# Attention's last chunks on one Trainium2 core: side columns copied ahead of one-hot matrices, one-hot matrices made by GpSimd, and residual sums placed behind the last gather

## The chip, the cores and the metric

The kernel runs on one core of one Trainium2 chip. The core has five engines that each work through their own queue in order: TensorE (PE, with its weight loads as PEld), VectorE (DVE), ScalarE (ACT), GpSimd (POOL) and SyncE (SP). They meet at semaphores. ACT, DVE and POOL compute on tiles of 128 partitions; POOL also issues the indirect DMAs (gathers) of this kernel, and SP issues its plain loads and stores. PE writes to PSUM, a small memory of banks; the other tiles live in SBUF.

The metric is the device time of one execution in microseconds. The kernel before takes 6164.96 us (median of 3 runs, 6163.35 to 6166.92).

## The reference, cut to what matters

A graph network with 6250 nodes of 128 features and 200,000 edges, sorted by destination. Two convolutions over the edges come first; then attention, whose end the change touches:

```python
q = (h @ qw + qb).reshape(n, H, HD)          # H = 8 heads, HD = 16
k = (h @ kw + kb).reshape(n, H, HD)
v = (h @ vw + vb).reshape(n, H, HD)
logits = (q[dst] * k[src]).sum(-1) * scale + (edge_attr @ ew + eb)
amax = jax.ops.segment_max(logits, dst, num_segments=n)
pe = jnp.exp(logits - amax[dst])
ssum = jax.ops.segment_sum(pe, dst, num_segments=n)
w = pe / jnp.clip(ssum[dst], 1e-06)
o = jax.ops.segment_sum(w[:, :, None] * v[src], dst, num_segments=n)
o = o.reshape(n, D) @ ow + ob
o = group_norm(o, an_g, an_b)
return h + o                                  # and the caller adds x
```

## The kernel before

**Chunks.** The edges are cut into 1563 columns of 128, and 8 columns make a chunk: 196 chunks, numbered 0 to 195, the last with 3 columns. For each chunk `fetch` (L1511) issues one plain load on SP and 8 gathers on POOL (L718, one indirect DMA of 128 rows of k and v for each column) into `k.g`, a ring of 11 buffers. The two convolutions before attention gather in the same way.

**First half of a chunk, in edge order.** PE multiplies the chunk's query rows with a one-hot matrix `ohT`, which ACT makes from loaded positions (`compared`, L685 and L686): the product `qe` has each edge's query and bias. `logits` multiplies it with the gathered keys on DVE (L1391), reduces over each head (L1395) and adds the bias `ebs`, which ACT copies out of PSUM (L1393), on DVE (L1397).

**Groups.** Chunks are grouped by 8, and at the end by 6, 5, 4 and 3 (`TAILS`, L37): 178 to 183, 184 to 188, 189 to 192 and 193 to 195. When a group's logits are there, `maxima` (L1409) turns them on PE (L1420), runs two scans on DVE (L1423, L1424), turns back (L1428), subtracts (L1432), takes the exponent on ACT (L1434, tile `pe`) and makes the end-of-run maxima `wl` on DVE (L1435).

**Second half, for the chunks of a finished group.** It runs one or two chunks a step, spread over the steps that the next group takes. For a chunk it needs
- a one-hot matrix `k.oh` of 128x1024 (edge by node of the window). DVE makes it in one instruction (L733, 173 times). For 23 chunks of the last 26 (`BY_ACT = 26`, L38) ACT makes it instead, a step ahead, in `early` (L1531): 8 squares (L1498) and one Relu (L1499);
- the tile `k.v` (`values`, L1572): ACT copies `pe` into every 17th column (L1444, inside `weighted`), DVE multiplies the gathered values with `pe` (L1445), and ACT copies `wl` and the end marks into 9 side columns (L1574, L1575). There are two buffers of `v`;
- the sums: 8 matmuls of `k.oh` with `k.v` on PE (L1452) into one of two PSUM tiles `us`;
- a merge with the running maxima `M` (`merge_late`, L1481: five small DVE instructions L1485, L1488, L1459, L1461, L1462, a copy L1463, and two exponents on ACT, L1465 and L1467), and one step later `add_late` (L1469 to L1477) into the running sums `flat`.

**What sets the order.** `pipeline` (L821) writes the steps out; `in_order` then fixes DVE, SP, ACT and PE to the order in which the Python code emits. POOL is not in that list (`ORDERED`, L17): a scheduler places its instructions by their dependencies. In step `n` the emitted order is: the fetch of chunk n+2, the second halves (`second`, L1541), the first half of chunk n, `values_ahead` for the next chunk (L1577), `compared` for chunk n+2, the products of chunk n+1, `early`, and then the piece of a batch of finished nodes (`attention_nodes`: copies `n_x` L908 and squares L919 on ACT, and others).

**After the chunks.** The last 9 windows of nodes need residuals: `h2` and `x` rows are loaded (`residuals`, L1016), `an_b` is added on POOL (L1606, one instruction of 128x1152), and x is added on POOL (`add_x`, L1027 and L1029). `last_nodes(3, hx[0])` then finishes those windows on DVE, ACT and PE.

Of the kernel before, what the change touches and what calls it, by code (L numbers as in the profile page):

```python
# [8 lines left out]
FP = mybir.dt.float32  # L9
# [3 lines left out]
ALU = mybir.AluOpType  # L13
# [8 lines left out]
P = 128  # L22
D = 128
H = 8
HD = 16
NT = 1
CH = NT * P
TPC = 8
# [22 lines left out]
def kernel(ctx: ExitStack, tc: tile.TileContext, x, src, dst, eat, w, out):  # L51
# [663 lines left out]
    def gather(k, g, table_d, ring=None):  # L715
        behind = None
        for t in range(k.nt):
            h = nc.gpsimd.indirect_dma_start(  # L718
                out=g[:, t, :table_d.shape[1]], out_offset=None, in_=table_d,
                in_offset=bass.IndirectOffsetOnAxis(ap=k.src[:, t:t + 1], axis=0))  # L720
            if ring is None:
                continue
            if behind is not None:
                tc.add_manual_dep(
                    h.ins, behind.name,
                    mybir.DependencyInfo(mybir.DependencyClass.NoSync, mybir.DependencyReason.DATA),
                    reason="one ring's order")
            behind = h.ins
            ring.mark(h, k.c, t, k.nt - 1)

    def onehot(k, pools, iota):
        k.oh = pools["oh"].tile([P, TPC, P], FP, name="oh")
# [609 lines left out]
    with ExitStack() as es:  # L1342
# [66 lines left out]
        def maxima(run, lg, nb, bp):  # L1409
# [27 lines left out]
            for j, k in enumerate(run):  # L1437
                k.pe, k.wl = pe[:, :k.nt, j, :], wl[:, :k.nt, j, :]

        def weighted(k):  # L1440

            k.v = vp.tile([P, TPC, VK + H + 1], FP, name="v", bufs=2)
            v4 = k.v[:, :, :VK].rearrange("p t (h c) -> p t h c", c=HD + 1)
            nc.scalar.copy(v4[:, :k.nt, :, HD], k.pe)  # L1444
            nc.vector.tensor_tensor(  # L1445
                v4[:, :k.nt, :, :HD], k.g[:, :k.nt, D:].rearrange("p t (h c) -> p t h c", c=HD),
                k.pe[:, :, :, None].to_broadcast([P, k.nt, H, HD]), ALU.mult)
# [47 lines left out]
        def onehot_by_act(k):  # L1495
# [2 lines left out]
                nc.scalar.activation(k.oh[:, t, :], iota_j, AF.Square, bias=k.dm[:, t:t + 1], scale=-1.0)  # L1498
            nc.scalar.activation(k.oh[:, :k.nt, :], k.oh[:, :k.nt, :], AF.Relu, bias=1.0, scale=-1.0)  # L1499

        class Stage:
            ahead, soon = 2, False
            sums, late, nb = [], [], None
# [7 lines left out]
            def fetch(self, c):  # L1511
                k = loads(c, pools, a_d[3], self.ahead)
                k.g = gp.tile([P, TPC, KV], FP, name="g")
                gather(k, k.g, kv_d, ring)
                return k

            def products(self, k):
# [12 lines left out]

            def early(self, ks, n, then):  # L1531

                for c in then[:2]:
                    if c >= NCH - BY_ACT:
                        onehot_by_act(ks[c])

            def root(self, run):
# [3 lines left out]
            def second(self, run, ks, first):  # L1541


                pieces = iter(())
                if run:
                    pieces = maxima(run, self.lg, self.nb, self.bp)
                    self.nb, self.j = None, 0
                for n, k in enumerate(ks):
                    mine = pieces if n == len(ks) - 1 else iter(())
                    next(mine, None)  # L1550
                    if k.oh is None:
                        onehot(k, pools, iota_of(k))
                    if self.sums:
                        self.sums[0].win = wins[self.sums[0].c]
                    next(mine, None)


                    if self.late:
                        add_late(self.late.pop(0))
                    if k.v is None:  # L1560
                        self.values(k)
                    sums(k, VK + H + 1)
                    next(mine, None)
                    self.values_ahead(ks[n + 1:] or self.then)
                    if self.sums:
                        merge_late(self.sums[0])
                        self.late.append(self.sums.pop())
                    self.sums.append(k)
                self.pieces = pieces
                return True  # L1570

            def values(self, k):  # L1572
                weighted(k)
                nc.scalar.copy(k.v[:, :k.nt, VK:VK + H], k.wl)  # L1574
                nc.scalar.copy(k.v[:, :k.nt, VK + H], ef[:, k.c * TPC:k.c * TPC + k.nt])  # L1575

            def values_ahead(self, ks):  # L1577

                for k in ks[:1]:
                    if k.pe is not None and k.v is None:  # L1580
                        self.values(k)

            def finish(self):
# [14 lines left out]
                add_late(self.sums[0])  # L1598

        with tc.tile_pool(name="bpa", bufs=1) as bp, tc.tile_pool(name="ohTa", bufs=2) as pools["ohT"]:  # L1600
            pipeline(3, Stage(bp))

        n = NW - NWD
        whole = min(n, FULL - NWD)
        hx = residuals(fin, NWD, n, whole, pool("xr", 1))
        nc.gpsimd.tensor_tensor(hx[0], hx[0], rows["an_b"][:, None, :].to_broadcast([P, n, D]), ALU.add)  # L1606
        add_x(nc.gpsimd, hx[0], hx[1], whole, n)

        pools["left"] = pool("left", 1)
# [3 lines left out]
        def left(k):  # L1613
            lp = pools["left"]
            left_rows(k, pools, a_d[3], bank)
            k.c = 0
            k.g = gp.tile([P, TPC, KV], FP, name="g")
            gather(k, k.g, kv_d)
            products(k, [(k.ohf.rearrange("p t e -> p (t e)"), k.rows), (k.ea, webl)])
            lg = lp.tile([P, TPC, H], FP, name="l_lg")  # L1620
            logits(k, lg)
            neg = lp.tile([P, 4, P], FP, name="l_neg")
            part = lp.tile([P, H, 2], FP, name="l_part")
            junk = lp.tile([P, 4, P], FP, name="l_junk")
            for a in range(2):
                nc.vector.tensor_scalar(neg, k.ohf[:, 4 * a:4 * a + 4, :], 1.0, BIG, ALU.subtract, ALU.mult)
                for h in range(H):
                    bc = bank()
                    for t in range(4):
                        nc.tensor.transpose(bc[:, t, :], lg[:, 4 * a + t, h:h + 1].to_broadcast([P, P]), ident)  # L1630
                    nc.vector.tensor_tensor_reduce(
                        junk, bc, neg, 1.0, -BIG, ALU.add, ALU.max, part[:, h, a:a + 1])
            cm = lp.tile([P, H], FP, name="l_cm")
            nc.vector.tensor_reduce(cm, part, AX.X, ALU.max)
            me = ps_.tile([P, TPC, H], FP, name="l_me", tag="pe")
            for t in range(TPC):
                nc.tensor.matmul(me[:, t, :], lhsT=k.ohf[:, t, :], rhs=cm, start=True, stop=True)
            nc.vector.tensor_tensor(lg, lg, me, ALU.subtract)

            nc.vector.tensor_scalar(lg, lg, 0.0, None, ALU.min)  # L1640
            k.pe = lp.tile([P, TPC, H], FP, name="l_pe")
            nc.scalar.activation(k.pe, lg, AF.Exp)
            weighted(k)
            sums(k, VK)
            tt = t3[:, bass.ds(k.win, 1), :]
            merge(k, M[:, bass.ds(k.win, 1), :], None, cm[:, None, :], 1)
            add(k, tt, 1)
# [43 lines left out]
```

## Time and profile before

| what | number |
|---|---|
| median of 3 runs | 6164.96 us |
| the profiled execution's own time | 6177.55 us |
| its span | 6175.8 us |
| mean granted PE clock | 0.75 |
| gathers on POOL, both convolutions | 3126, 950 ns each |
| gathers on POOL, attention | 1563, 954 ns each |
| last gather issued | 6064.52 us from the start |

The profile is of one execution. The groups give, for instructions of one line, engine and shape, the busy time, the mean duration and the idle time of the engine just before them with what ended it. The timeline gives single instructions: start, duration, engine, line, operation, tiles, count, and in brackets the idle time before. All times below are microseconds from the start of the span unless they say otherwise. The profiled execution took 12.6 us longer than the median of the runs.

### The profile page before, as it was taken

Reading aid. Unit: us, or ns where it says so; the run is one execution under the profiler, and the core shown is the slowest. Engines: PE = TensorE matmul, PEld = TensorE weight load, DVE = VectorE, ACT = ScalarE, POOL = GpSimd, SP = SyncE. Lnnn points to the kernel's source line nnn. Section 1 sums busy time; section 2 is a strip of 40 time slices with the busy share of each in tenths; the row PEclk is TensorE's granted clock in tenths of the full one; section 3 lists DMA queues with packets and bytes.
Section 4 is the critical chain, followed back from the end, with each engine's and each line's share of the span. In section 5 each row is a group of like instructions: output and inputs, shape, how many; then the busy total and the mean of one; then the engine's idle time right before and its main releaser. Section 6 shows DMA issues by size and latency. Waiting matters only on the chain. (4 is left out here: it accounts for less than half of the span.)

```text
span 6175.8 us, 68330 instructions
## 1 busy us (share of the span) xinstructions
PE 3615.7 (59%) x20941; PEld 3418.9 (55%) x20942; DVE 4994.3 (81%) x7118; ACT 3353.9 (54%) x5295; POOL 4487.6 (73%) x4706
## 2 busy tenths in 40 slices
PE   5555556556556455565565656555655666666555
PEld 4555555555555455555555555544555555555555
DVE  7888888888888578777888888856778888888877
ACT  5666666666666566666666666632333333333354
POOL 5777777777777577777777777757777777777772
PEclk8777667777777677777777787766778777777776
DMA  6444344444433333343344444445566666666652
GB/s 160 116 127 121 96 115 105 102 108 107 107 101 101 80 100 96 100 101 100 102 114 114 109 112 108 112 121 146 152 157 162 165 166 163 163 166 162 165 150 62
DMA packets 391221, 758.87 MB, mean 123 GB/s; under 512 B 89647, under 2 KB 256946, under 8 KB 361441
## 3 DMA queue, kind: packets, MB, share of 16 engines
q0 software_dynamic: 175056, 410.03, 25.9%
q1 hardware_dynamic: 210144, 340.73, 21.0%
q10 hardware_dynamic: 5632, 3.50, 0.2%
q8 instruction: 173, 2.83, 0.2%
q14 instruction: 216, 1.77, 0.1%
HBM read 707.34 MB, written 46.58 MB: 122 GB/s over the span
## 5 line engine op out<-in xcount | busy, mean ns | idle before, releaser
L718 POOL DMA_INDIRECT g<-b_d,src_i x3126 | 2970.9, 950 | 963.4 <-issue 915.5
L1198 PE MATMUL u<-h,oh 128*128 128x129 f32 (+1 forms) x6252 | 1266.3, 384 | 1435.0 <-ACT h L1193 1434.9
L1198 PEld LDWEIGHTS u<-h,oh 128*128 128x128 f32 x6252 | 1169.3, 288 | 1517.1 <-ACT h L1193 1512.6
L718 POOL DMA_INDIRECT g<-kv_d,src_i x1563 | 1490.7, 954 | 494.6 <-issue 446.4
L1166 PE MATMUL m<-pk,ohT 101*128 101x128 f32 x6252 | 943.2, 315 | 206.4 <-DVE h L1173 161.9
L1166 PEld LDWEIGHTS m<-pk,ohT 101*128 101x128 f32 x6252 | 909.7, 231 | 227.3 <-DVE h L1173 180.7
L1173 DVE TENSOR_TENSOR h<-m,g 128x1024 f32<-128x1024 f32 x392 | 476.4, 1215 | 519.4 <-DMA g<-b_d,src_i 496.0
L1452 PE MATMUL us<-v,oh 128*128 128x145 f32 x3126 | 593.1, 359 | 385.4 <-DVE flat L1477 340.6
L1376 PE MATMUL qe<-pk,ohT 101*128 101x136 f32 x3126 | 567.1, 352 | 373.7 <-ACT ebs L1393 364.1
L1452 PEld LDWEIGHTS us<-v,oh 128*128 128x128 f32 x3126 | 549.8, 250 | 425.6 <-DVE flat L1477 239.6
L1376 PEld LDWEIGHTS qe<-pk,ohT 101*128 101x128 f32 x3126 | 525.0, 252 | 406.5 <-ACT ebs L1393 399.8
L1193 ACT ACTIVATE h<-h 128x1024 f32<-128x1024 f32 x392 | 413.0, 1054 | 594.4 <-DVE h L1192 578.9
L1175 ACT ACTIVATE sq<-h 128x1024 f32<-128x1024 f32 x392 | 411.7, 1050 | 527.9 <-DVE h L1173 526.0
L685 ACT ACTIVATE ohT<-ohT,minus_p 96x1024 f32<-96x1024 f32 x588 | 669.2, 1138 | 17.0 <-DMA ohT<-rel_d 16.5
L686 ACT ACTIVATE ohT<-ohT 96x1024 f32<-96x1024 f32 x588 | 619.8, 1054 | 18.7
L1177 DVE TENSOR_REDUCE var<-sq 128x64 f32<-128x1024 f32 x392 | 475.0, 1212 | 104.5 <-ACT sq L1175 104.4
L1191 DVE TENSOR_TENSOR h<-h,cps 128x1024 f32<-128x1024 f32 x392 | 477.1, 1217 | 13.5
L1192 DVE TENSOR_TENSOR h<-h,cps 128x1024 f32<-128x1024 f32 x392 | 477.0, 1217 | 13.4
L733 DVE TENSOR_TENSOR oh<-cps,dm 128x1024 f32<-128x1024 f32 x392 | 474.2, 1210 | 2.1 <-PE u L1198 2.1
L1188 DVE TENSOR_TENSOR h<-h,cps 128x1024 f32<-128x1024 f32 x392 | 473.7, 1208 | 0.0
L1391 DVE TENSOR_TENSOR g<-qe,g 128x768 f32<-128x768 f32 (+1 forms) x391 | 251.1, 683 | 235.0 <-DMA g<-kv_d,src_i 234.6
L1465 ACT ACTIVATE us<-d 128x16 f32<-128x16 f32 x196 | 36.7, 187 | 660.0 <-DVE d L1461 605.6
(286 smaller groups left out, 4270.6 us busy)
## 6 DMA issues: line engine op xcount, KB each, us to landing
ohT<-rel_d SPq DMA_DIRECT2D x291, 768.0 KB
g<-b_d,src_i POOLq DMA_INDIRECT x3126, 2.5
pk<-a_d SPq DMA_DIRECT2D x588, 46.0 KB
g<-kv_d,src_i POOLq DMA_INDIRECT x1563, 3.0
ohT<-in_eat_dram SPq DMA_DIRECT2D x291, 40.0 KB
a_d<-n_o SPq DMA_DIRECT2D x28, 256.0 KB
kv_d<-n_o SPq DMA_DIRECT2D x28, 256.0 KB
n_h<-h_d SPq DMA_DIRECT2D x19, 256.0 KB
```

Source lines behind the costliest of these rows:

```text
L685: nc.scalar.activation(k.ohT[:WN, :], k.ohT[:WN, :], AF.Square, bias=minus_p[:WN])
L686: nc.scalar.activation(k.ohT[:WN, :], k.ohT[:WN, :], AF.Relu, bias=1.0, scale=-4.0)
L718: h = nc.gpsimd.indirect_dma_start(out=g[:, t, :table_d.shape[1]], out_offset=None, in_=table_d, in_offset=bass.IndirectOffsetOnAxis(ap=k. ...
L733: return nc.vector.tensor_tensor(k.oh[:, :k.nt, :], iota[:, None, :].to_broadcast([P, k.nt, P]), k.dm[:, :, None].to_broadcast([P, k.nt, P ...
L1166: nc.tensor.matmul(k.m[:, t, :], lhsT=lhs[:, t * P:(t + 1) * P], rhs=rhs, start=(j == 0), stop=(j == len(terms) - 1))
L1173: nc.vector.tensor_tensor(k.mt, k.m[:, :n], k.g[:, :n], ALU.add)
L1177: return lambda: nc.vector.tensor_reduce(var[:, at:at + n * H], sq[:, :n].rearrange("p t (g c) -> p (t g) c", c=HD), AX.X, ALU.add)
L1191: nc.vector.tensor_tensor(k.mt, k.mt, over_edges(gam, k.nt), ALU.mult)
L1192: nc.vector.tensor_tensor(k.mt, k.mt, over_edges(bet, k.nt), ALU.add)
L1198: nc.tensor.matmul(k.u[:, 0, :wide], lhsT=k.oh[:, t, :], rhs=k.h[:, t, :wide], start=(t == 0), stop=(t == k.nt - 1))
L1376: nc.tensor.matmul(k.qe[:, t // TB, at:at + DB], lhsT=lhs[:, t * P:(t + 1) * P], rhs=rhs, start=(j == 0), stop=(j == len(terms) - 1))
L1452: nc.tensor.matmul(k.u[:, :wide], lhsT=k.oh[:, t, :], rhs=k.v[:, t, :wide], start=(t == 0), stop=(t == k.nt - 1))
```

## The change

Three edits, all in attention.

**1. Side columns.** `weighted` is split: `columns(k)` takes a buffer of `v` and copies `pe` into it, and the stage's `columns` adds the `wl` and end-mark copies. `early` calls it for the chunk after the last one whose values are done (`done + 1`), ahead of the one-hot matrices that it emits. `done` replaces the test on `k.v`. On ACT this changes the order alone: wherever the three copies stood behind the one-hot matrices or behind a batch's `n_x` copy or squares, they now stand ahead of them. That is so at 34 places in the middle of attention (behind `n_x` alone) and in nearly all steps of the last 26 chunks. The order on PE, DVE and SP is the same as before.

**2. One-hot matrices by GpSimd.** In the last three steps with chunks (n + 2 >= 195) `early` calls `onehot_by_pool`: 8 instructions of 128x128 on POOL for each chunk, tied behind the last gather that has been emitted. In the built program these are 4 chunks, 189 to 192, so 32 instructions; the 4 chunks' 36 instructions on ACT are gone. The last three, 193 to 195, are still made by DVE (L733), as before.

**3. Residual sums.** The sum of `an_b` on POOL is tied behind the last gather. Before, the scheduler had put it among the gathers, behind the 105th gather of attention; now the order on POOL is: last gather, sum of `an_b`, the 32 one-hot instructions, sums of `x`.

```diff
@@ gather
             behind = h.ins
             ring.mark(h, k.c, t, k.nt - 1)
+        return behind
+
+    def follows(h, behind):
+        tc.add_manual_dep(
+            h.ins, behind.name,
+            mybir.DependencyInfo(mybir.DependencyClass.NoSync, mybir.DependencyReason.DATA),
+            reason="behind the gathers")
+        return h
@@ values of a chunk
-        def weighted(k):
-
-            k.v = vp.tile([P, TPC, VK + H + 1], FP, name="v", bufs=2)
-            v4 = k.v[:, :, :VK].rearrange("p t (h c) -> p t h c", c=HD + 1)
-            nc.scalar.copy(v4[:, :k.nt, :, HD], k.pe)
+        def heads(k):
+            return k.v[:, :, :VK].rearrange("p t (h c) -> p t h c", c=HD + 1)
+
+        def columns(k):
+            k.v = vp.tile([P, TPC, VK + H + 1], FP, name="v", bufs=2)
+            nc.scalar.copy(heads(k)[:, :k.nt, :, HD], k.pe)
+
+        def weighted(k):
+            v4 = heads(k)
             nc.vector.tensor_tensor(
@@ one-hot matrices
+        def onehot_by_pool(k, behind):
+            k.oh = pools["oh"].tile([P, TPC, P], FP, name="oh")
+            for t in range(k.nt):
+                follows(nc.gpsimd.tensor_scalar(
+                    k.oh[:, t, :], iota_j, k.dm[:, t:t + 1], None, ALU.is_equal), behind)
@@ fetch
-                gather(k, k.g, kv_d, ring)
+                self.behind = gather(k, k.g, kv_d, ring)
@@ early
+                k = ks.get(self.done + 1)
+                if k is not None and k.pe is not None:
+                    self.columns(k)
                 for c in then[:2]:
-                    if c >= NCH - BY_ACT:
+                    if n + self.ahead >= NCH - 1:
+                        onehot_by_pool(ks[c], self.behind)
+                    elif c >= NCH - BY_ACT:
                         onehot_by_act(ks[c])
@@ second
-                    if k.v is None:
+                    if k.c > self.done:
                         self.values(k)
@@ values, values_ahead
+            done = -1
+
+            def columns(self, k):
+                if k.v is None:
+                    columns(k)
+                    nc.scalar.copy(k.v[:, :k.nt, VK:VK + H], k.wl)
+                    nc.scalar.copy(k.v[:, :k.nt, VK + H], ef[:, k.c * TPC:k.c * TPC + k.nt])
+
             def values(self, k):
+                self.columns(k)
                 weighted(k)
-                nc.scalar.copy(k.v[:, :k.nt, VK:VK + H], k.wl)
-                nc.scalar.copy(k.v[:, :k.nt, VK + H], ef[:, k.c * TPC:k.c * TPC + k.nt])
+                self.done = k.c
...
-                    if k.pe is not None and k.v is None:
+                    if k.pe is not None and k.c > self.done:
                         self.values(k)
@@ after the chunks
-            pipeline(3, Stage(bp))
+            stage = Stage(bp)
+            pipeline(3, stage)
...
-        nc.gpsimd.tensor_tensor(hx[0], hx[0], rows["an_b"][:, None, :].to_broadcast([P, n, D]), ALU.add)
+        follows(nc.gpsimd.tensor_tensor(
+            hx[0], hx[0], rows["an_b"][:, None, :].to_broadcast([P, n, D]), ALU.add), stage.behind)
@@ chunks outside the steps
+            columns(k)
             weighted(k)
```

## The prediction

> **What bounds the kernel now.** I read the table of stretches first, then DVE's groups in the stretch before the ACT one-hot matrices and in the stretch with them, then the timeline around the last.
>
> ```profile
> core 0: us, PE busy (x) PEld busy (x) DVE busy (x) ACT busy (x) POOL busy (x), PEclk, DMA share, GB/s
> 5000.00:5800.00 800.00, 488.46 (x2823) 455.71 (x2822) 685.39 (x1418) 288.39 (x775) 606.50 (x635) 0.79 0.63 164
> 5900.00:6066.00 166.00, 101.37 (x527) 94.10 (x527) 117.81 (x267) 102.41 (x289) 125.53 (x132) 0.71 0.57 151
> 6066.00:6155.00 89.00, 50.82 (x267) 46.72 (x266) 68.12 (x166) 43.78 (x137) 2.77 (x2) 0.71 0.08 21
> ...
> L1391 DVE TENSOR_TENSOR g<-qe,g 128x768 f32<-128x768 f32 x79 | 75.3, 954 | 58.0 <-DMA g<-kv_d,src_i 57.6 <-PE us L1452 0.3
> L1423 DVE TENSOR_TENSOR_SCAN blk<-nbs,blk 64x1024 f32<-64x1024 bf16 x10 | 22.9, 2287 | 18.3 <-PE blk L1420 18.3
> ...
> L718 POOL DMA_INDIRECT g<-kv_d,src_i x132 | 125.6, 951 | 40.2 <-issue 38.1 <-DVE flat L1477 0.6 <-DVE blk L1423 0.6
> L1445 DVE TENSOR_TENSOR v<-g,pe 128x1024 f32<-128x1024 f32 x25 | 30.5, 1220 | 52.1 <-ACT v L1444 52.1
> L1391 DVE TENSOR_TENSOR g<-qe,g 128x768 f32<-128x768 f32 x17 | 16.2, 951 | 0.0
> ```
>
> From 5000 to 5800 DVE has 85% of the time busy, and what it waits for is gathered rows (57.6 us, L1391). POOL issues gathers without a stop: 635 in 800 us, one every 1.26 us. So POOL's issue sets the pace. From 5900 to the end (the last three rows) L1391 waits no more: rows lie ready. DVE now waits 52.1 us ahead of L1445, for the side-column copies on ACT, and falls behind. At 6066 the gathers are over and DVE still needs 89 us. A wait in this last stretch is paid in full, and a gap in the gathers before it too.
>
> **Residual sum (edit 3).**
>
> ```profile
> 4217.99 0.95 POOL L718 DMA_INDIRECT g<-kv_d,src_i  x1 [0.30 <-issue]
> 4226.06 2.62 POOL L1606 TENSOR_TENSOR n_h<-n_h,r_an_b 128x1152 f32<-128x1152 f32 x1 [7.12 <-issue]
> 4228.86 1.19 POOL L718 DMA_INDIRECT g<-kv_d,src_i  x1 [0.18 <-issue]
> ...
> 6064.52 0.94 POOL L718 DMA_INDIRECT g<-kv_d,src_i  x1 [0.30 <-issue]
> ```
>
> A gather ends at 4218.94 and the next starts at 4228.86: 9.92 us where 0.30 is usual. The page does not say what the 7.12 us were; they leave the gather stream either way, so all later gathers, and with them DVE until 5900, come 9.6 us earlier. That is term A, **9.6 us**. Bounds: 2.6 if the 7.12 us return within the gathers, 9.9 at most. Its load of `h2` on SP does not move. It passes 1458 gathers on POOL and is needed only by the last sums on DVE, so at its new place it can only hold up what is queued behind it: the one-hot matrices (below) and the sums of x, which wait for a later load in any case.
>
> **Side columns (edit 1).** In the middle of attention the swap with a batch's copy changes nothing: DVE's wait for rows covers it, and without that cover it would be worth 0.5 us a place. In the last stretch there are two kinds of steps. A step with one ACT one-hot matrix:
>
> ```profile
> 6068.90 2.43 ACT L1498 ACTIVATE oh<-iota_j,dm 128x128 f32<-128x128 f32 x8
> 6071.36 1.06 ACT L1499 ACTIVATE oh<-oh 128x1024 f32<-128x1024 f32 x1
> 6072.61 1.22 DVE L1445 TENSOR_TENSOR v<-g,pe 128x1024 f32<-128x1024 f32 x1 [2.93 <-ACT v L1444]
> 6077.28 0.23 DVE L1397 TENSOR_TENSOR lg<-l,ebs 128x64 f32<-128x64 f32 x1
> ...
> 5951.62 1.22 DVE L1445 TENSOR_TENSOR v<-g,pe 128x1024 f32<-128x1024 f32 x1 [1.20 <-ACT v L1444]
> 6012.67 1.22 DVE L1445 TENSOR_TENSOR v<-g,pe 128x1024 f32<-128x1024 f32 x1 [4.56 <-ACT v L1444]
> 6082.55 1.22 DVE L1445 TENSOR_TENSOR v<-g,pe 128x1024 f32<-128x1024 f32 x1 [2.95 <-ACT v L1444]
> ```
>
> The matrix takes ACT 3.4 us. With the copies ahead of it DVE starts L1445 at once and has 4.7 us of work (6072.61 to 6077.28) before it next needs ACT, for `ebs`. So the wait goes. There are 8 such waits from 5951.62 to 6082.55, 20.6 us in all: the 52.1 us less 29.5 of the five steps below, and less 2.0 of five waits of 0.4 us, which stand right behind a group's exponent and stay. One of them (4.56) has two table loads of 1.28 us and a root of 0.32 us behind its matrix; 3.4 + 2.9 + 0.35 for `ebs` is 6.7 against 4.7, so 1.9 us of it comes back at L1397. **18.7 us.**
>
> A step with two:
>
> ```profile
> 6051.50 2.43 ACT L1498 ACTIVATE oh<-iota_j,dm 128x128 f32<-128x128 f32 x8
> 6057.39 1.06 ACT L1499 ACTIVATE oh<-oh 128x1024 f32<-128x1024 f32 x1
> 6058.35 0.57 ACT L908 COPY n_x<-blk 128x512 f32<-128x512 f32 x1
> 6058.81 0.28 ACT L1444 COPY v<-pe 128x64 f32<-128x64 f32 x1
> 6059.13 1.22 DVE L1445 TENSOR_TENSOR v<-g,pe 128x1024 f32<-128x1024 f32 x1 [7.09 <-ACT v L1444]
> 6060.87 0.17 DVE L1461 TENSOR_TENSOR d<-M,mn 128x16 f32<-128x16 f32 x1
> 6061.08 0.19 ACT L1465 ACTIVATE us<-d 128x16 f32<-128x16 f32 x1 [1.80 <-DVE d L1461]
> 6061.66 0.44 DVE L1471 TENSOR_TENSOR flat<-flat,us 128x272 f32 x1 [0.41 <-ACT v L1444]
> 5921.56 1.22 DVE L1445 TENSOR_TENSOR v<-g,pe 128x1024 f32<-128x1024 f32 x1 [4.14 <-ACT v L1444]
> 5938.10 1.22 DVE L1445 TENSOR_TENSOR v<-g,pe 128x1024 f32<-128x1024 f32 x1 [5.05 <-ACT v L1444]
> 5997.92 1.22 DVE L1445 TENSOR_TENSOR v<-g,pe 128x1024 f32<-128x1024 f32 x1 [6.01 <-ACT v L1444]
> 6108.68 1.22 DVE L1445 TENSOR_TENSOR v<-g,pe 128x1024 f32<-128x1024 f32 x1 [7.16 <-ACT v L1444]
> ```
>
> Here the wait is moved on rather than removed. After L1445 and the merge, 1.9 us, DVE needs the exponent L1465, and that stands behind both matrices. Now: matrices done 6058.45, copy `n_x`, columns, L1445, merge, exponent, L1471 at 6061.66. Then: columns first, matrices done 0.45 later, `n_x`, exponents 0.3, L1471 at about 6059.7. Gain 1.9 us. Five steps are of this kind (4.14, 5.05, 6.01, 7.09, 7.16); four keep their matrices on ACT: 4 x 1.9 = **7.6 us**. Bounds 4 (L1471 still late) and 22.3 (all of the four waits).
>
> The new order also adds a wait on ACT: with two buffers of `v` the early copies must wait for the sums of the chunk two before, and the one-hot matrices queue behind them. Where the sums run late that is up to one chunk's sums, 2.2 to 4.2 us (the last fence), but DVE is then held by the same sums today. I take it as nothing.
>
> **One-hot matrices by POOL (edit 2).** The fifth double step (7.16, chunks 189 and 190) loses both from ACT; what stays of its wait is what a group's first chunk waits, about 0.5 us. **6.5 us.** The other two matrices (chunks 191 and 192) stand before no DVE wait. No POOL row has this instruction, so its price is bounded by others of about its size:
>
> ```profile
> masks.py:199 POOL TENSOR_SCALAR_AFFINE_SELECT ident<-ident 128x128 f32<-128x128 f32 x1 | 0.3, 287 | 0.0
> masks.py:197 POOL MEMSET ident<- 128x128 f32 x1 | 0.2, 205 | 0.3 <-POOLq L1677 0.3
> L1029 POOL TENSOR_TENSOR n_h<-n_h,n_xr 106x128 f32<-106x128 f32 x1 | 0.5, 462 | 0.0
> ```
>
> One input and one output, like the 287 ns row: 0.3 us each, 2.4 us a chunk, ends 0.2 and 0.46. With gathers over at 6055.8, 7.1 us of idle time again and 2.62 us for the sum, the 32 start at 6065.7; at 0.3 us nothing waits for them (first rival).
>
> **What comes back.** Two terms. First, a DVE that is not late meets PE again: from 5000 to 5800 each scan L1423 waited 1.8 us for PE's transposes (18.3 over 10), while the five scans after 5900 wait 2.3 in all. I expect some 6.8 instead: **-4.5 us** (bounds 0 and -6.8). Second, POOL and DVE get in each other's way:
>
> ```profile
> 4226.97 1.79 DVE L1397 TENSOR_TENSOR lg<-l,ebs 128x64 f32<-128x64 f32 x1
> 6137.32 2.35 POOL L1027 TENSOR_TENSOR n_h<-n_h,n_xr 128x1024 f32<-128x1024 f32 x1 [71.85 <-DVE us L1475]
> 6139.16 0.54 DVE L1459 TENSOR_TENSOR mn<-cm,M 128x16 f32<-128x16 f32 x1
> ```
>
> L1397 ended at 4228.76, just when the POOL sum ended (4228.68), and L1459 at 6139.70, with L1027; L1391 and L1395 beside the first were not slowed. So a DVE instruction with both inputs in SBUF waits for a POOL one. Each chunk has five small ones (L1397, L1459, L1461, L1462, L1463). Over four chunks at 0 to 0.3 us each that is 0 to 6, plus 0 to 2.6 for the sum: I take **-3 us**.
>
> The Trainium skill (SBUF — State Buffer, "Who interferes with whom") says why: a VectorE instruction with two SBUF inputs contends with a GpSimd instruction that reads SBUF, and the later one blocks until the first has ended. The two rows agree; by that rule at its worst the term is the -8.6 above. The same skill (GPSIMD Engine Reference, "Engine selection") says that one-input GpSimd work runs roughly at line rate, which speaks for the low end of the price; no run here shows it.
>
> **The sum.** 9.6 + 18.7 + 7.6 + 6.5 - 4.5 - 3.0 = 34.9 us. The profiled execution's 6177.55 becomes 6142.7; I carry the difference over to the median: 6164.96 - 34.9 = **6130 us** (0.57% faster). No change that this kernel's measurement can tell means within 0.2%, 12.3 us: 6152.6 to 6177.3.
>
> **The rivals.**
>
> *POOL's matrices are too slow (the slower side).* Place: the sums of chunk 192, the last POOL chunk.
>
> ```profile
> 6127.62 2.22 PE L1452 MATMUL us<-v,oh 128*128 128x145 f32 x16 [0.41 <-DVE flat L1477]
> 6121.41 4.21 PE L1452 MATMUL us<-v,oh 128*128 128x145 f32 x16 [3.86 <-DVE flat L1477]
> ```
>
> They start at 6127.62 today and, with all terms ahead of them, at about 6092. The 32 instructions end at 6065.7 + 32p, so from p = 0.8 us on each further 0.1 costs 3.2 us; at 1.9 nothing is left of the gain, and at 2.4 the kernel is 14 us slower: 6179. The three POOL rows (0.2 to 0.46) speak against; for it, that POOL has not run this instruction here. Chance 4% for slower, 3% for between.
>
> *The wait only changes its name.* PE's sums need the same one-hot matrices, and DVE's merge needs the sums; if that chain sets the pace, edit 1 gives the 1.9 us in each of its 8 + 4 steps, 22.8, of which the scans take 6.8; edit 2, whose matrices stand in the same chain, gives nothing. 9.6 + 16.0 - 3.0 = 22.6: 6142. For it: PE's granted clock is 0.71 there and its sums take 2.2 or 4.2 us. Against: from 5900 to 6155 DVE is busy for 185.9 us over the 25 full chunks, some 7 us a chunk, and a chunk's matrix takes ACT 3.4 us. Chance 15%.
>
> *The gap in the gathers doesn't count,* because DVE is late anyway by the end: 34.9 - 9.6 gives 6140. For it: no wait for rows after 5900. Against: DVE's lateness starts only there. Chance 7%.
>
> *The change doesn't reach the path at all:* 6165. The 52.1 us are on DVE with no other wait left, so 4%.
>
> **How the numbers follow.** The forecast has 67%. The range reaches from nothing coming back (34.9 + 7.5, rounded: 6122) to the second rival with the worst POOL term (8.6 for 3): 6147. Faster by over 0.2%: 67 + 15 + 7 + 1 = 90%; within: 6%; slower: 4%.
>
> **What would show it.** In the profile after: the gap at 4218.94 is 0.3 us and the last gather starts near 6055; L1445's idle time falls from 52.1 to under 8 us, and L1471 shows 12 to 18 us of waits for ACT in the four double steps; L1391's stays near 0 in the last stretch; the POOL instructions take 0.2 to 0.46 us and no PE sum waits for POOL; L1459 and its kind take up to 0.5 us while they run; from the last gather to the last L1477 it is some 63 us where it is 88 now. I am wrong if L1452 or L1423 take over more than 10 us of the removed wait, or if the POOL instructions take over 0.8 us.

## The result, and the profile after

| | before | after |
|---|---|---|
| median of 6 runs each | 6165.94 us (6163.35 to 6168.76) | 6129.62 us (6126.32 to 6134.86) |
| ratio | | 0.9938, 95% interval 0.9928 to 0.9947 |
| the profiled execution | 6177.55 us | 6127.41 us |
| last gather to last add of attention, start to start | 88.1 us | 63.0 us |

The change saves 36.3 us (33 to 44 by the interval of the ratio); the forecast was 34.9 and 6130. The last adds of attention before and after, for the last row of the table:

```profile
6152.59 0.44 DVE L1477 TENSOR_TENSOR flat<-flat,us 128x272 f32 x1
...
6102.42 0.44 DVE L1489 TENSOR_TENSOR flat<-flat,us 128x272 f32 x1
```

The edits moved the line numbers: L1391, L1395, L1397 are now L1399, L1403, L1405; L1423 is L1431; L1444 and L1445 are L1453 and L1457; L1452 is L1464; L1459, L1461 are L1471, L1473; the exponent L1465 is L1477, and the add's products L1471 and L1477 are L1483 and L1489; L1498 and L1499 are L1510 and L1511.

The two profiled executions differ by 50 us, more than the medians. The first gather of attention starts at 4076.69 us where it was 4088.98, in front of which nothing was edited, and a gather of attention takes 952 ns on the mean where it was 954: some 15 us of the 50 are not the change's.

In ten of the twelve runs described below, on three chips, every kernel, the one before too, took some 8000 us with PE's granted clock at 0.67 to 0.68 instead of 0.75, and PE, DVE, ACT and SP repeatedly stood still together while POOL went on gathering (last section); of these runs the end of attention is read, and what POOL pays for its first computing instruction.

The table of stretches of the changed kernel (busy time and instruction count of each engine), with the last gathers in the second row and what follows them in the third:

```profile
5000.00:5800.00 800.00, 493.59 (x2829) 460.81 (x2827) 685.23 (x1420) 287.47 (x775) 606.55 (x636) 0.78 0.63 164
5875.00:6041.00 166.00, 106.39 (x610) 100.61 (x609) 133.99 (x304) 117.68 (x330) 125.42 (x132) 0.77 0.58 155
6041.00:6105.00 64.00, 34.81 (x193) 31.74 (x192) 54.83 (x131) 17.23 (x63) 24.70 (x35) 0.72 0.06 19
```

In the middle nothing moved (685 us of DVE in 800 in both). Over the last gathers DVE now works 134.0 of 166 us where it worked 117.8, and it needs 64 us after them instead of 89. Its groups from 5875 to 6105:

```profile
L1457 DVE TENSOR_TENSOR v<-g,pe 128x1024 f32<-128x1024 f32 x25 | 30.4, 1217 | 3.1 <-ACT v L1453 3.1
L1399 DVE TENSOR_TENSOR g<-qe,g 128x768 f32<-128x768 f32 x17 | 16.2, 951 | 0.0
L1471 DVE TENSOR_TENSOR mn<-cm,M 128x16 f32<-128x16 f32 x28 | 6.8, 244 | 1.0
```

Its waits there (line, what it waited for, us in all, times, the longest):

```profile
DVE flat L1483 <- ACT us L1477: 15.0, 4, 5.3
DVE blk L1431 <- PE blk L1428: 7.2, 4, 3.3
DVE v L1457 <- ACT v L1453: 3.1, 7, 0.5
DVE lg L1405 <- ACT ebs L1401: 2.0, 1, 2.0
```

Before, the waits ahead of the same add and the same scans were these (5900 to 6155):

```profile
DVE blk L1423 <- PE blk L1420: 2.2, 2, 1.5
DVE flat L1471 <- ACT v L1444: 0.8, 2, 0.4
```

The 52.1 us ahead of the product of the values are 3.1, and the chunks' rows still lie ready (L1399, no idle time). What came back has three names: exponents in four double steps (15.0), transposes ahead of the scans (7.2), one `ebs` (2.0).

POOL's timeline, at the place where the residual sum stood (the trace before has it behind the 104th gather of attention, not the 105th; here the 104th starts at 4205.48, and the 105th is shown) and at the end:

```profile
4206.73 0.95 POOL L718 DMA_INDIRECT g<-kv_d,src_i  x1 [0.30 <-issue]
...
6039.40 0.95 POOL L718 DMA_INDIRECT g<-kv_d,src_i  x1 [0.30 <-issue]
6047.88 2.61 POOL L1638 TENSOR_TENSOR n_h<-n_h,r_an_b 128x1152 f32<-128x1152 f32 x1 [7.53 <-issue]
6050.48 9.28 POOL L1516 TENSOR_SCALAR oh<-iota_j,dm 128x128 f32<-128x128 f32 x16
6062.12 10.05 POOL L1516 TENSOR_SCALAR oh<-iota_j,dm 128x128 f32<-128x128 f32 x16 [2.35 <-PE us L1464]
```

From the list of the sum's own line (POOLq is POOL's queue):

```profile
L1638 POOLq MODIFY_POOL_CONFIG  x2: 43/43/43, 6040.4 to 6040.4; - x2
```

The gap is gone: 0.30 us. The idle time ahead of the sum went with it (7.53 at the new place), behind two instructions that change POOL's configuration. A one-hot instruction takes 9.28 / 16 = 0.58 us, and 0.63 in the second half, twice what was forecast.

### The profile page after: what moved, and what is told of

Its sections match the earlier page's. It is cut to its first block, busy times and chain, and to the rows that moved or that the text cites. A ratio compares the mean times of both kernels' runs of the same rounds, so it can differ in the third digit from the quotient of the medians.

```text
span 6125.2 us, 68319 instructions
## 1 busy us (share of the span) xinstructions
PE 3621.9 (59%) x20941; PEld 3430.7 (56%) x20942; DVE 4995.8 (82%) x7118; ACT 3339.8 (55%) x5259; POOL 4498.1 (73%) x4738
## 5 line engine op out<-in xcount | busy, mean ns | idle before, releaser
L1206 PE MATMUL u<-h,oh 128*128 128x129 f32 (+1 forms) x6252 | 1282.2, 388 | 1424.2 <-ACT h L1201 1424.1
L1206 PEld LDWEIGHTS u<-h,oh 128*128 128x128 f32 x6252 | 1182.9, 291 | 1505.8 <-ACT h L1201 1501.0
L1464 PE MATMUL us<-v,oh 128*128 128x145 f32 x3126 | 585.1, 355 | 354.4 <-DVE flat L1489 309.5
L1464 PEld LDWEIGHTS us<-v,oh 128*128 128x128 f32 x3126 | 541.5, 247 | 394.3 <-DVE flat L1489 226.9
L685 ACT ACTIVATE ohT<-ohT,minus_p 96x1024 f32<-96x1024 f32 x588 | 669.2, 1138 | 16.8 <-DMA ohT<-rel_d 16.8
L1399 DVE TENSOR_TENSOR g<-qe,g 128x768 f32<-128x768 f32 (+1 forms) x391 | 251.2, 684 | 227.9 <-DMA g<-kv_d,src_i 227.6
L1477 ACT ACTIVATE us<-d 128x16 f32<-128x16 f32 x196 | 36.6, 187 | 649.2 <-DVE d L1473 575.3
```

Source lines behind the costliest of these rows:

```text
L685: nc.scalar.activation(k.ohT[:WN, :], k.ohT[:WN, :], AF.Square, bias=minus_p[:WN])
L1206: nc.tensor.matmul(k.u[:, 0, :wide], lhsT=k.oh[:, t, :], rhs=k.h[:, t, :wide], start=(t == 0), stop=(t == k.nt - 1))
L1464: nc.tensor.matmul(k.u[:, :wide], lhsT=k.oh[:, t, :], rhs=k.v[:, t, :wide], start=(t == 0), stop=(t == k.nt - 1))
```

## The experiments

Three switches make the kernels with some of the edits: edit 1 out, edit 2 out, edit 3 out.

```diff
-                if k is not None and k.pe is not None:
+                if False:
                     self.columns(k)
...
-                    if n + self.ahead >= NCH - 1:
+                    if False:
                         onehot_by_pool(ks[c], self.behind)
...
-        follows(nc.gpsimd.tensor_tensor(
-            hx[0], hx[0], rows["an_b"][:, None, :].to_broadcast([P, n, D]), ALU.add), stage.behind)
+        nc.gpsimd.tensor_tensor(hx[0], hx[0], rows["an_b"][:, None, :].to_broadcast([P, n, D]), ALU.add)
```

Where a run took 8000 us, the stretch from the start of the reduce of chunk 189 (L1403) to the start of the last add is compared; it has the fourth double step and the steps of edit 2 in it:

```
                              189 to last add   189 to 190 (fourth double step)
before                        106.0             20.0
residual sum alone            105.7             20.0
POOL's matrices alone          99.2             20.0
columns alone                  99.1, 97.5       17.8, 17.8   (6144 and 8000 us)
changed, no POOL matrices      98.6, 100.5      18.9, 19.6   (both 8000 us)
changed, no residual edit      93.5             17.8
changed                        95.0             17.8
two small POOL instructions    92.9             17.8
POOL's matrices twice          96.5, 94.9       19.4, 19.0   (both 8000 us)
second matrix later            92.1             16.8
first matrix by DVE            93.5             14.3
```

Each number is one start less another, for "POOL's matrices alone" 7947.59 - 7848.43. The first two rows agree, 106.0 in a run of 6178 us and 105.7 in one of 8000, so the stretch can be read; but the three kernels that ran twice differ by 1.6 to 1.9 us from themselves, so it is good to some 2 us.

**Columns alone.** Edits 2 and 3 are out.

> Edit 1 alone (side columns ahead of the one-hot matrices; all one-hot matrices stay on ACT; the an_b sum among the gathers). The forecast: 18.7 for the single steps, five double steps at 1.9, less 4.5 for the scans = 23.7 us faster, about 6142; from the last gather to the last add 64 to 66 us where it was 88; DVE's idle time ahead of its product of the values under 8 us, its waits ahead of the add's first product 16 to 23 us in five double steps; the gap of 9.9 us among the gathers is still there. The rival (the wait only changes its name, PE's sums and the merges set the pace): 13 steps at 1.9 less 6.8 = 17.9 us faster, about 6148, 70 us from the last gather to the last add, and waits for PE ahead of the merges in most steps.

The first run took 7995.83 us against 8016.01 (ratio 0.9967, 0.9951 to 0.9983). The second:

> Edit 1 alone once more (side columns ahead of the one-hot matrices; all matrices of the last 26 chunks but the last three on ACT; the an_b sum among the gathers), on a chip of its own, since the eight runs so far took 8000 us where the kernel before had 6166. If the chip paces the kernel as in the two profiles of before and after: the forecast's 23.7 us faster, ratio 0.9962; 64 to 66 us from the last gather to the last add; DVE's idle time ahead of its product of the values under 8 us, its waits ahead of the add's first product 16 to 23 us in five double steps; the gap of 9.9 us among the gathers. The rival (the wait only changes its name): 17.9 us, ratio 0.9971, 70 us from the last gather to the last add. If the kernel takes 8000 us again, DVE waits for rows right up to the last chunks and neither number can be read.

6144.36 us against 6168.90: ratio 0.9961 (0.9947 to 0.9974), 24.5 us faster where 23.7 were forecast. DVE's waits from 5900 to 6122:

```profile
DVE flat L1483 <- ACT us L1477: 22.2, 5, 7.0
DVE blk L1431 <- PE blk L1428: 4.2, 3, 2.4
DVE v L1457 <- ACT v L1453: 2.1, 5, 0.4
```

Its timeline at the sum, at the last gather and at the last add:

```profile
4218.75 2.62 POOL L1638 TENSOR_TENSOR n_h<-n_h,r_an_b 128x1152 f32<-128x1152 f32 x1 [7.21 <-issue]
...
6055.08 0.95 POOL L718 DMA_INDIRECT g<-kv_d,src_i  x1 [0.30 <-issue]
6119.74 0.44 DVE L1489 TENSOR_TENSOR flat<-flat,us 128x272 f32 x1
```

From the last gather to the last add it is 6119.74 - 6055.08 = 64.7 us: the forecast said 64 to 66, the rival 70. The interval of the ratio holds both; the trace tells them apart. In the single steps no wait took the removed one's place, and the five double steps hold 22.2 us.

**The residual sum alone (edits 1 and 2 out), and the change without it (edit 3 out).**

> Edit 3 alone (the an_b sum behind the last gather; side columns and one-hot matrices as before). The forecast's term A: the gap of 9.92 us among the gathers falls to 0.30, the last gather comes 9.6 us earlier, and from the start of the last gather to the last add of attention it stays 88 us, or 89 with the POOL sum now beside DVE's last work: 8.5 to 9.6 us faster, about 6157. The rival (DVE is late by the end anyway, the gap does not count): last gather 9.6 us earlier, but 97 to 98 us from there to the last add, 6166.

> The changed kernel without edit 3 (the an_b sum stays among the gathers). The forecast: the gap of 9.9 us is back, the last gather 9.6 us later, and 62 to 63 us from there to the last add as in the changed kernel: 8.5 to 9.6 us slower than it, about 6139. The rival (the gap does not count): from the last gather to the last add 53 us, 6130.

Both took 8000 us: ratios 0.9995 (0.9981 to 1.0008) and 0.9971 (0.9954 to 0.9987). POOL's gathers wait for buffers in these runs, some 56 us just at the sum's old place, so neither time nor place of the last gather answers. No run of 6100 us has edit 3 alone or leaves only it out; what it is worth is a difference between the two that differ in edits 2 and 3. The gathers of attention took 1973 us with the sum among them (columns alone, 4081.9 to 6055.1) and 1963 in the changed kernel, while the time behind the last gather went from 64.7 to 63.0 us. Edit 2's 4 us (next) lie in that time too, so with edit 3 some 2.4 us came back there; the rival, by which the gap does not count, needs 10 to come back. That leaves edit 3 some 7 of its 9.6 us; the medians leave 36.3 - 24.5 - 4 = 7.8, with intervals of several us.

**POOL's matrices alone (edits 1 and 3 out), and the change without them (edit 2 out, two runs).**

> Edit 2 alone (the one-hot matrices of chunks 189 to 192 by POOL; side columns behind ACT's matrices as before; the an_b sum among the gathers). The forecast: the wait of 7.16 us in the fifth double step falls to about 0.5 = 6.5 us, less 0.5 to 1.5 for DVE instructions held by POOL's: 5 to 6 us faster, about 6160, 82 to 83 us from the last gather to the last add. The rival (the chain of matrices and sums sets the pace, edit 2 gives nothing): 0 us, 6166, 88 us. By the changed kernel's profile POOL should take 0.59 us for each of the 32, not 0.3.

> The changed kernel without edit 2 (ACT makes the matrices of chunks 189 to 192). The forecast: edit 2 is worth 6.5 less the 1.9 that edit 1 gives in that step, less some 0.6 us of DVE instructions held by POOL: 4 us slower than the changed kernel, about 6134, and 67 us from the last gather to the last add where the changed kernel has 63. The rival (edit 2 gives nothing): 6130 and 63 us.

> The changed kernel without edit 2 once more (ACT makes the matrices of chunks 189 to 192), on a chip of its own. The forecast: edit 3 adds 9.6 us less some 1 us (the sum now stands beside DVE's last work) to the 24.5 us that edit 1 alone gave, so 33 us faster than the kernel before; edit 2 is worth 6.5 - 1.9 - 0.6 = 4 us on top, so 4 us slower than the changed kernel: ratio 0.9946, 66 us from the last gather to the last add where the changed kernel has 63. The rivals: edit 2 gives nothing (ratio 0.9941, 63 us); the gap in the gathers does not count (the last gather 9.6 us earlier, 74 us from there to the last add, ratio 0.9960).

All three took 8000 us (ratios 0.9997, 0.9985 to 1.0009; 0.9981, 0.9968 to 0.9995; 0.9964, 0.9949 to 0.9980): too wide for 4 or 6 us. The end of attention answers. Alone, edit 2 takes 106.0 (105.7) to 99.2: 6.6 to 6.9 us, forecast 6.5 less up to 1.5. On top of edit 1 it is worth 99.1 - 95.0 = 4.1 in the 6100-us runs (which differ in edit 3 too), and 97.5 - 93.5 = 4.0 in the two 8000-us runs that differ in nothing else; forecast 4. The changed kernel without it has 98.6 and 100.5. The rival, by which it gives nothing, falls: all these differences have the same sign and are larger than the 2 us.

**Two small POOL instructions among the gathers.**

```diff
+                if c in (60, 100):
+                    t = wk.tile([P, P], FP, name="spare", bufs=1)
+                    h = nc.gpsimd.tensor_scalar(t, iota_j, iota_j[:, 0:1], None, ALU.is_equal)
+                    self.behind = follows(h, self.behind).ins
```

> The changed kernel with two more POOL instructions of 128x128 (a compare into a tile that nobody reads), one tied behind the gathers of chunk 60, one behind those of chunk 100. Theory 1 (the 7.12 us idle ahead of the an_b sum is what POOL needs to go from gathers to computing, whatever it computes): two gaps of 7.1 + 0.6 + 0.6 = some 8.3 us, the last gather 16 us later, 16 us slower than the changed kernel, about 6146. Theory 2 (the idle time belongs to that sum, its load or its place): two gaps of 0.9 to 1.2 us, 1 to 2 us slower, about 6131.

Neither theory came out. The time says nothing (8003 us); POOL's timeline does, at the first, at the second and behind the last gather (no bracket: no idle time ahead):

```profile
5991.60 0.61 POOL L1535 TENSOR_SCALAR spare<-iota_j 128x128 f32<-128x128 f32 x1 [7.04 <-issue]
...
6549.80 0.64 POOL L1535 TENSOR_SCALAR spare<-iota_j 128x128 f32<-128x128 f32 x1
...
7891.40 2.63 POOL L1642 TENSOR_TENSOR n_h<-n_h,r_an_b 128x1152 f32<-128x1152 f32 x1
```

And the list of the added line:

```profile
L1535 POOLq MODIFY_POOL_CONFIG  x2: 43/43/43, 5984.6 to 5984.7; - x2
```

The first pays 7.04 us behind the two configuration instructions, which belong to it alone; the second and the sum itself pay nothing. It is neither the sum's own nor a price of each switch from gathers to computing: it is paid once, by whichever computing instruction comes first.

**Each POOL instruction twice.**

```diff
-                follows(nc.gpsimd.tensor_scalar(
+                for _ in range(2):
+                    follows(nc.gpsimd.tensor_scalar(
...
```

> The changed kernel with each of the 32 POOL instructions issued twice, so that a slice of a matrix costs 1.2 us instead of 0.59. The first rival's mechanism (POOL's matrices late for the sums of chunk 192): 64 instructions from 6050.5 end at 6088 or, with the 2.4 us wait for a buffer, 6091, where PE begins those sums at 6077.8 and ends them at 6080: 8 to 12 us slower than the changed kernel, 6138 to 6142, with PE waiting for POOL in the trace. If POOL's matrices are covered further than I think: under 2 us slower, 6130 to 6132.

> The changed kernel with each of the 32 POOL instructions issued twice once more (1.2 us a slice instead of 0.6), on a chip of its own. The first rival's mechanism: in the changed kernel POOL's matrices end at 6072.2 and PE begins the sums of chunk 192 at 6077.8, so some 5.6 us are to spare; 19 us more make PE wait, 8 to 12 us slower than the changed kernel, ratio 0.9951 to 0.9958, from the last gather to the last add 71 to 75 us instead of 63, and DVE waits for PE's sums ahead of a merge. If the matrices are covered further than I think: ratio 0.9938 to 0.9941, 63 to 65 us.

Both took 8000 us (ratio 0.9968 in both, 0.9952 to 0.9985 and 0.9949 to 0.9987). The second's timeline at the end, POOL and then PE:

```profile
7913.45 18.52 POOL L1517 TENSOR_SCALAR oh<-iota_j,dm 128x128 f32<-128x128 f32 x32 [18.14 <-PE us L1464]
7932.65 19.98 POOL L1517 TENSOR_SCALAR oh<-iota_j,dm 128x128 f32<-128x128 f32 x32 [0.68 <-PE us L1464]
...
7928.35 6.54 PE L1464 MATMUL us<-v,oh 128*128 128x145 f32 x32 [1.14 <-DVE flat L1489]
7948.61 2.27 PE L1464 MATMUL us<-v,oh 128*128 128x145 f32 x12 [1.20 <-POOL oh L1517]
7952.10 1.09 PE L1464 MATMUL us<-v,oh 128*128 128x145 f32 x4 [1.21 <-POOL oh L1517]
```

POOL's matrices end at 7952.63 and PE now waits for them in the last sums: these go on to 7953.19, 4.6 us where they take 2.2 in the changed kernel, so some 2.4 us more. The stretch of the table is no longer than in the changed kernel (94.9 and 96.5 against 95.0). That does not settle the threshold: here POOL begins 14.9 us ahead of the first sums (7913.45 to 7928.35), in the changed kernel's profile 7.3 (6050.48 to 6057.81, next section). With 7.6 us less of a lead PE would wait some 10 us; that is an estimate, and at 6100 us it was not measured.

**Second matrix behind the exponents.** ACT makes the second matrix of a double step in the loop of `second`, behind the merge in between:

```diff
-                for c in then[:2]:
+                for c in then[:2] if n + self.ahead >= NCH - 1 else then[:1]:
...
                     if k.oh is None:
-                        onehot(k, pools, iota_of(k))
+                        if n and NCH - BY_ACT <= k.c < NCH - 3:
+                            onehot_by_act(k)
+                        else:
+                            onehot(k, pools, iota_of(k))
```

> The changed kernel with the second ACT matrix of each double step placed behind the exponents of the merge in between. Theory 1 (what is left in the double steps, 15.0 us in four waits, is the exponent's place behind both matrices and nothing else): each wait loses the 3.4 us of one matrix, 13.6 us, about 6116. Theory 2 (PE's sums of the step's first chunk, which start when its matrix is done and take 4.2 us, stand right behind that wait): 1 to 4 us faster than the changed kernel, 6126 to 6129, and DVE waits for PE ahead of the merge and for ACT's columns ahead of its product of the values instead.

8000 us again (ratio 0.9964, 0.9948 to 0.9980). The fourth double step went from 17.8 to 16.8 us. DVE's timeline there:

```profile
7899.43 0.44 DVE L1483 TENSOR_TENSOR flat<-flat,us 128x272 f32 x1 [1.72 <-ACT us L1477]
7903.47 1.22 DVE L1457 TENSOR_TENSOR v<-g,pe 128x1024 f32<-128x1024 f32 x1 [2.38 <-ACT v L1453]
```

The wait of 5.30 us ahead of the add (next section) is now 1.72 and 2.38. The second is for the next columns, which stand behind the second matrix and then wait 0.21 us more on ACT for PE's sums; without the matrix the sums would hold them as long. That is theory 2, 1 us in this step; its wait for PE ahead of the merge did not show, and the other three double steps were not read.

**First matrix by DVE.** In double steps DVE makes the first matrix; the one-hot matrices on POOL stand ahead of the sum; and a multiply on POOL was to draw the configuration change ahead:

```diff
+    nc.gpsimd.tensor_scalar(M, M, 1.0, None, ALU.mult)
...
-                for c in then[:2]:
+                for c in then[:2] if n + self.ahead >= NCH - 1 else then[-1:]:
                     if n + self.ahead >= NCH - 1:
-                        onehot_by_pool(ks[c], self.behind)
+                        self.behind = onehot_by_pool(ks[c], self.behind)
```

> The changed kernel with three more edits: DVE makes the first matrix of each double step (one instruction of 1.22 us) and ACT only the second; a POOL instruction of one multiply by 1 stands ahead of all gathers of attention, so that POOL's change of configuration (two instructions, then 7.0 us idle) is paid where POOL waits anyway; the 32 POOL one-hot instructions stand ahead of the an_b sum. Theory 1 (the 15.0 us left in the four double steps are ACT's second matrix ahead of the exponents; with one matrix of 3.4 us less they go, against four times 1.22 us on DVE; the POOL matrices, ready 7.5 + 2.6 us earlier, do not become the next wait): 13.6 - 4.9 + 2 = some 11 us faster than the changed kernel, ratio 0.9920, 52 to 54 us from the last gather to the last add, DVE's waits ahead of the add's first product under 4 us, and no 7 us of idle time ahead of POOL's first instruction behind the last gather. Theory 2 (PE's sums take the wait over, as in the rival of the changed name): 0 to 5 us faster, 58 to 63 us, waits for PE ahead of the merges.

6125.98 us against 6167.53: ratio 0.9934 (0.9921 to 0.9948), 41.6 us faster; theory 1's ratio, 0.9920, lies just outside. DVE's waits from 5880 to 6102 (lines are one higher here):

```profile
DVE v L1458 <- ACT v L1454: 7.8, 9, 3.7
DVE blk L1432 <- PE blk L1429: 5.3, 4, 1.8
DVE flat L1484 <- ACT us L1478: 0.9, 2, 0.8
```

Its timeline, POOL at the end and the last add:

```profile
6044.91 0.95 POOL L718 DMA_INDIRECT g<-kv_d,src_i  x1 [0.30 <-issue]
6052.89 19.59 POOL L1517 TENSOR_SCALAR oh<-iota_j,dm 128x128 f32<-128x128 f32 x32 [7.03 <-issue]
...
6098.93 0.44 DVE L1490 TENSOR_TENSOR flat<-flat,us 128x272 f32 x1
```

The exponents' wait went from 15.0 to 0.9 us, and it is 54.0 us from the last gather to the last add: theory 1. In two points it failed. POOL's matrices did become a wait: with DVE that much earlier, PE's weight loads wait for them eleven times (12.2 us by the list of waits), ACT's columns wait 4.96 us for those sums, and DVE waits 3.7 for the columns. And the multiply did nothing for the 7.03 us: the scheduler put it at 7.85 us, ahead of an all-reduce on POOL at 54.33, and they stayed. The stretch behind the gathers is 9 us shorter than in the changed kernel; the time can't tell the two apart, as their intervals overlap.

## Why the prediction was right, point by point

- **What bounds the kernel.** Gathers until 5900, then DVE's waits, paid in full: right. Behind the last gather it took 63.0 us, forecast 63.
- **Residual gap, 9.6 us:** 9.92 to 0.30 is 9.62. Which way the 7.12 us would go was left open; they left the gathers with the sum. Some 2.4 us came back behind the last gather; a part of that is the term of POOL and DVE below. Edit 3's share is known as a difference alone, from no run of its own.
- **Single steps 18.7, double steps 7.6, fifth double step 6.5, together 32.8.** The profile has 52.1 - 3.1 = 49.0 us off ahead of the product of the values, 15.0 - 0.8 = 14.2 back at the add and 2.0 at the `ebs` sum (forecast 1.9): 32.8. The four double steps held 22.3 us of waits and hold 15.0: 7.3 gained, forecast 7.6. One of them, ACT and then DVE:

```profile
6012.76 2.45 ACT L1510 ACTIVATE oh<-iota_j,dm 128x128 f32<-128x128 f32 x8
6015.24 1.06 ACT L1511 ACTIVATE oh<-oh 128x1024 f32<-128x1024 f32 x1
6016.20 2.43 ACT L1510 ACTIVATE oh<-iota_j,dm 128x128 f32<-128x128 f32 x8
6020.09 0.19 ACT L1477 ACTIVATE us<-d 128x16 f32<-128x16 f32 x1
...
6014.84 0.17 DVE L1475 COPY M<-mn 128x16 f32 x1
6020.31 0.44 DVE L1483 TENSOR_TENSOR flat<-flat,us 128x272 f32 x1 [5.30 <-ACT us L1477]
```

  DVE is through with its merge at 6015.0 and stands until the exponent has passed both matrices, 6020.3.
- **Two buffers of `v`, taken as nothing:** right. ACT's columns do wait for PE's sums, as foreseen (6.8 us in seven waits, before 1.7 in one), but DVE's waits for the columns are seven of at most 0.5 us.
- **Scans, -4.5 us:** 2.2 to 7.2 us of waits, -5.0.
- **POOL and DVE, -3 us:** L1471 takes 244 ns on the mean where the same line (L1459) took 190, 28 times: -1.5 us. Two that lie beside POOL's sum and beside a one-hot instruction:

```profile
6049.25 1.27 DVE L1471 TENSOR_TENSOR mn<-cm,M 128x16 f32<-128x16 f32 x1
6059.11 0.45 DVE L1471 TENSOR_TENSOR mn<-cm,M 128x16 f32<-128x16 f32 x1
```

  The line's group before the change, from 5900 to 6155:

```profile
L1459 DVE TENSOR_TENSOR mn<-cm,M 128x16 f32<-128x16 f32 x28 | 5.3, 190 | 1.0
```

  The first ended at 6050.52, with the sum (6050.49). The other four lines took the same as before to 0.2 us in all. The mechanism was right, the term half of what was taken: the forecast had four chunks' small instructions beside POOL's work, and only three of the 28 merges fell into it. (One of the five lines it named, the copy, has one input, not two.)
- **POOL's price, 0.3 us: wrong, and outside its bounds (0.2 to 0.46).** It is 0.58 to 0.63. The row it was taken from has 128x128, one input and one output too, but another operation. It cost nothing, because the rival's threshold, 0.8 us, was near the truth: 6050.5 + 32p meets PE's sums of chunk 192 (the last PE row here) at p = 0.85. The 2.35 us of waiting for a buffer do not add to that, as they are gone from p = 0.73 on.

```profile
6057.81 6.69 PE L1464 MATMUL us<-v,oh 128*128 128x145 f32 x32 [1.14 <-DVE flat L1489]
6071.62 4.21 PE L1464 MATMUL us<-v,oh 128*128 128x145 f32 x16 [4.45 <-POOL oh L1516]
6077.84 2.22 PE L1464 MATMUL us<-v,oh 128*128 128x145 f32 x16 [0.88 <-DVE flat L1489]
...
6071.04 0.44 DVE L1489 TENSOR_TENSOR flat<-flat,us 128x272 f32 x1
```

  POOL ended at 6072.2, 5.7 us ahead of the sums of chunk 192. The profile puts PE's 4.45 us ahead of the sums of chunk 191 down to POOL, against the forecast's sign that no sum waits for it; but they start 0.14 us after the end of DVE's add (6071.04 + 0.44), as the other two rows start 0.14 and 0.15 us after theirs, so it was the add. The 4% for the slower side were too few for a price that was off by two. The Trainium skill (GPSIMD Engine Reference, "Engine selection") was read as speaking for the low end; 128 elements a partition in 0.59 us, where DVE makes 1024 in 1.22, do not bear that out, though one size does not separate a rate from a fixed cost.
- **The rivals.** The changed name fell with the columns alone (64.7 us behind the last gather, not 70) and with edit 2's 4.1 and 6.6 us. It is right in a small part: moving the second matrix gives 1 us of 5.3. The gap that does not count fell by 1973 against 1963 us of gathers, of which some 2.4 and not 10 came back.
- **What was luck.** The measured terms, 9.6 + 32.8 - 5.0 - 1.5, give 35.9 us, and the forecast missed the median's 36.3 by 1.4, with 33 to 44 as its interval: the mechanism was right, so close a hit is partly chance. POOL's price, off by two, would have cost time had DVE been earlier, as the run with the first matrix by DVE shows.

## What to carry to other kernels

A wait that is the only one left on the bounding engine was worth its full size here, but go through the next two places where that engine needs the same queue: single steps gave nearly all of their waits, double steps a third, because an exponent stood behind the same matrices. A price taken from a row of the same shape but another operation can be off by two, so the bound needs that width and the cover has to be worked out. Where medians can't resolve a few us, start-to-start times over a short stretch can, here to some 2 us: run a kernel twice to learn how far.

## What the runs showed of the hardware

- The first computing instruction on POOL after an all-reduce (at 53 to 54 us) and thousands of gathers pays 6.9 to 7.8 us of idle time, once, behind two configuration instructions, in every run. That the all-reduce draws it was not tested by a run. The Trainium skill (GPSIMD Engine Reference, "Instruction dispatch") gives about 6 us for the first call of code that has to be loaded; the two traces whose configuration instructions are shown above have 6.9 (5984.7 to 5991.60) and some 7.4 (6040.4 and two times 0.043, to 6047.88).
- POOL's residual sum held a DVE instruction of 0.17 us for 3.24 us in the run with two small instructions, until the sum's end (7891.40 + 2.63), though by the profile it started 0.57 us ahead of the sum; the prediction has the later one wait:

```profile
7890.83 3.24 DVE L1473 TENSOR_TENSOR d<-M,mn 128x16 f32<-128x16 f32 x1
```

- In the runs of 8000 us there are stretches like this one (the sum alone; engines in the order of the first table):

```profile
5120.00:5156.00 36.00, 0.22 (x2) 0.00 (x0) 0.00 (x0) 0.00 (x0) 27.18 (x29) 0.55 0.37 107
```

  POOL issues 29 gathers and their packets move, and PE, DVE and ACT do nothing for 36 us. What holds them was not found.
